# Layer 1's output by rows, and the gates' products back on TensorE, in a four-layer graph network

## The chip, the cores and the metric

The kernel runs on one core of a Trainium2 chip. The metric is the device time of one execution in microseconds, the median of several runs. A core has TensorE (matrix products, PE in the profile), VectorE (DVE), ScalarE (ACT), GpSimd (POOL) and SyncE (SP, which issues transfers). Each engine works through its own instructions in order and waits on semaphores for the others. The on-chip memories are SBUF, for operands, and PSUM, into which TensorE writes its sums.

## The reference

Sixteen graphs (B) with 1024 nodes (N) of 128 features (D), each with a dense 1024 x 1024 adjacency of zeros and ones, go through four layers with residual sums and layer norms between them. Cut to what matters here:

```python
# layer 0: graph attention with one gate
h = x @ W_w.T + W_b
e = (h @ A) @ h.T;  e = e + e.T
att = softmax(where(adj > 0, e, -9e15), axis=1) * adj
hp = relu(att @ h)
coeff = sigmoid(concat([x, hp]) @ gate_w.T + gate_b)      # gate_w: 1 x 256
x1 = layernorm(x + coeff * x + (1 - coeff) * hp)

# layer 1: the adjacency is thinned row by row (dilation), then three steps
for l in 1, 2, 3:
    agg = adj_d @ h / deg
    out = agg @ Wr_l + h @ Wx_l + b_l
    out = out / max(norm(out, axis=-1), 1e-12) * mask
    h = batchnorm(relu(out), g_l, be_l)                   # over all graphs and nodes
x2 = layernorm(x1 + (concat([h1, h2, h3]) @ Wl + bl) * mask)

# layer 2: graph attention with three gates (ig, fg, og: 1 x 256 each, over concat([x, hp]))
# layer 3: two normalised propagations over adj + I, between ELUs
```

A gate's product over `concat([x, hp])` is the sum of a product of `x` with the first 128 weights and one of `hp` with the last 128.

## The kernel before

The program goes stage by stage over all 16 graphs: layer 0; the dilation; the three steps of layer 1; then layers 2 and 3 together. Within a stage the work of neighbouring graphs is interleaved: while graph b is in its attention, graph b+1 is prepared (`before`) and graph b-1 is finished (`after`). The build then orders each engine's instructions. NT is 8, the number of blocks of 128 nodes; H2 is 2, the number of halves of 512. The adjacency as f32 rows comes in 512 KB transfers through two buffers (`an`).

```python
# helpers: a "half" is one PSUM buffer of 128 x 512; "turned" is a transpose by TensorE
def products(psum, *pairs):                 # output by columns: weights stay, x moves
    for p, c, _ in halves(psum):
        for i, (W, x) in enumerate(pairs):
            nc.tensor.matmul(p, W, x[:, c], start=(i == 0), stop=(i == len(pairs) - 1))   # L765
        yield p, c

def gate(out, x, g, tmp):                   # layer 0's gate product with x
    nc.gpsimd.tensor_tensor(tmp, x, g[:, None, :].to_broadcast([P, NT, P]), op=OP.mult)   # L771
    for n in (64, 32):
        nc.gpsimd.tensor_tensor(tmp[:, :, :n], tmp[:, :, :n], tmp[:, :, n:2 * n], op=OP.add)   # L773
    nc.vector.tensor_reduce(out, tmp[:, :, :32], AX.X, OP.add)                            # L774

def normed(small, r):                       # layer norm: VectorE statistics, GpSimd power, ScalarE scale
    ...
    rstd = power_mhalf(small, mv[:, :, 1], add=LN_EPS, name="ln_rstd")                    # L744
    nc.vector.scalar_tensor_tensor(nb, ...)                                               # L790
    for i in range(NT): nc.scalar.activation(r[:, i, :], r[:, i, :], AF.Identity, ...)    # L792
```

Layer 0, where a graph is prepared in eight parts (`it` = 0 to 7), one to each block of adjacency rows. Turns, products and the gate share two PSUM buffers (`ps_h`):

```python
# each part: adjacency rows to bf16 (L904), checked (L907), turned by TensorE (L911), stored as fp8 (L912)
if it == 1:   xT = turned x
elif it == 3: s.hT = W0T, xT products
elif it == 5:
    s.G = ...
    gate(s.gx, s.xn, gxr, work.tile([P, NT, P], F32, name="r"))
elif it == 7: s.hn = turned hT
...
# attention, per block: pmm = hT . G (L723), mask and maximum (L946), exp (L950),
# hs = hn / sum (L954), acc += hs . em (L957)
# after: pz = 8 products of hpT with gw (L966), co = pz + gx, tanh, mix with x, layer norm
```

Layer 1's output, per graph and step:

```python
def out(self, b):
    oT = work.tile([P, N], F32, name="oT")
    for p, c in products(ps_h, (self.Wx, st.hT), (self.Wr, st.ag)):
        nc.scalar.activation(oT[:, c], p, AF.Identity, bias=self.bcol)                    # L1374
    ...
    for p, c, k in turned(*((ps_a, oT, "acc") if self.l == 2 else (ps_h, oT))):           # L758
        nc.scalar.activation(oT[:, c], p, AF.Square)                                      # L1379
        nc.vector.tensor_reduce(ss[:, k], tiles3(oT[:, c]), AX.X, OP.add)                 # L1380
        turns.append((p, k))
    ...
    rn = power_mhalf(small, ss, floor=1e-24, name="rn")
    ...
    for p, k in turns:
        nc.vector.scalar_tensor_tensor(st.n[:, k, :], tiles3(p), 0.0, half_rows(rn[:, k]), ...)   # L1387
# then keep: n turned (L758), evicted (L1396), statistics (L1397), stored; and for steps one and two
# the adjacency product of n in two parts, hi and lo (L1274), scaled into ag (L1406)
```

Layers 2 and 3: the gates' products with x are VectorE's, three gates by eight blocks:

```python
# before: yT, layer norm of xn, then
xT = wide("xT", 2);  turned xn, copied by ScalarE                                         # L1530
for g in range(3):
    for i in range(NT):
        nc.vector.scalar_tensor_tensor(small.tile([P, P], BF16, name="gtmp"), s.xn[:, i, :], 1.0, l2.gxr[g],
                                       op0=OP.mult, op1=OP.mult, accum_out=s.gx[:, g, i:i + 1])   # L1534
s.hT = W2T . xT;  s.G = As2 . hT;  s.hn = turned hT
...
# after: pg = 8 products of hpT with gw (3 columns, L1586); gt = pg + gb (L1588); gt += gx (L1589); tanh (L1590);
# the gated mix, layer norm; U0 product, two ELUs (L1483 to L1485, L1479 to L1481), U1 product (L1494),
# propagation hi and lo (L1508), prop (L1510), ELU, U2 product, propagation, turned back (L758, L1641), layer norm
```

Of the kernel before, what the change touches and what calls it, by code (L numbers as in the profile page):

```python
# [22 lines left out]
P = 128  # L23
# [616 lines left out]
def fast_kernel(ctx: ExitStack, tc: tile.TileContext, t: dict, out: bass.AP, flag: bass.AP):  # L640
# [34 lines left out]
    bad = consts.tile([P, 2, NT, B], BF16, name="bad")  # L675
# [13 lines left out]
    def row_bcast(pool, src, n, name):  # L689

        v = pool.tile([P, n], F32, name=name)
        nc.sync.dma_start(v, bass.AP(tensor=src.tensor, offset=src.offset, ap=[[0, P], [1, n]]))
        return v
# [6 lines left out]
    def matrix(pool, src, name):  # L700
        v = pool.tile([P, P], F32, name=name)
        nc.sync.dma_start(v, src)
        return v
# [63 lines left out]

    def gate(out, x, g, tmp):


        nc.gpsimd.tensor_tensor(tmp, x, g[:, None, :].to_broadcast([P, NT, P]), op=OP.mult)  # L771
        for n in (64, 32):
            nc.gpsimd.tensor_tensor(tmp[:, :, :n], tmp[:, :, :n], tmp[:, :, n:2 * n], op=OP.add)  # L773
        nc.vector.tensor_reduce(out, tmp[:, :, :32], AX.X, OP.add)  # L774
# [100 lines left out]
    with ExitStack() as ph:  # L875
# [11 lines left out]
        gxr = row_bcast(wts, t["L0_gnn_gate_w"][0, :P], P, "l0gxr")  # L887
        gw = column(wts, t["L0_gnn_gate_w"][0, P:], "l0gw")
# [6 lines left out]
        def before(s, b):  # L895
# [3 lines left out]
            for it in range(NT):  # L899
# [13 lines left out]
                if it == 1:  # L913
                    xT = work.tile([P, N], F32, name="xT")
                    for p, c, _ in turned(ps_h, s.xn):
                        nc.scalar.copy(xT[:, c], p)
                elif it == 3:
                    s.hT = work.tile([P, N], F32, name="hT", bufs=2)
                    for p, c in products(ps_h, (W0T, xT)):
                        nc.scalar.activation(s.hT[:, c], p, AF.Identity, bias=b0)  # L920
                elif it == 5:
                    s.G = work.tile([P, N], F32, name="G", bufs=2)
                    for p, c in products(ps_h, (As0, s.hT)):
                        nc.scalar.copy(s.G[:, c], p)
                    s.gx = small.tile([P, NT], F32, name="gx")
                    gate(s.gx, s.xn, gxr, work.tile([P, NT, P], F32, name="r"))
                elif it == 7:
                    s.hn = work.tile([P, N], F32, name="hn")
                    for p, c, _ in turned(ps_h, s.hT):
                        nc.vector.tensor_copy(s.hn[:, c], p)  # L930
# [29 lines left out]
        def after(s, b):  # L960
# [4 lines left out]
            for i in range(NT):  # L965
                nc.tensor.matmul(pz[:, i:i + 1], hpT[:, i * P:(i + 1) * P], gw, start=True, stop=True)  # L966
# [205 lines left out]
    class Layers23:  # L1172
# [8 lines left out]
        def weights(self, ps_h):  # L1181
# [7 lines left out]
            self.gxr = []  # L1189
            self.gw = wts.tile([P, 3], F32, name="l2gw")  # L1190
            self.gb = wts.tile([P, 3], F32, name="l2gb")
            for i, n in enumerate(("ig", "fg", "og")):
                w, src = t[f"L2_gnn_{n}_w"], t[f"L2_gnn_{n}_b"]
                self.gxr.append(row_bcast(wts, w[0, :P], P, f"l2gxr{i}"))
                nc.sync.dma_start(self.gw[:, i:i + 1], bass.AP(tensor=w.tensor, offset=w.offset + P, ap=[[1, P], [1, 1]]))
# [31 lines left out]
    with ExitStack() as ph:  # L1227
# [50 lines left out]
        class Step:  # L1278


            def __init__(self, l, before):
                s = str(l + 1)
                self.l = l
                self.Wr = matrix(wts, t[f"L1_gnn_Wr{s}"], f"Wr{s}")
                self.Wx = matrix(wts, t[f"L1_gnn_Wx{s}"], f"Wx{s}")
                self.bcol = column(wts, t[f"L1_gnn_b{s}"], f"b{s}")
# [8 lines left out]
            def take_norm(self):  # L1295
# [4 lines left out]
                pc = ps_h.tile([P, 1], F32, name="pc", tag="h")  # L1300
                nc.tensor.matmul(pc, ws, ab[:, 1:2], start=True, stop=True)
                nc.vector.tensor_add(self.bcol, self.bcol, pc)
# [66 lines left out]
            def out(self, b):  # L1369

                st = self.batches[b]
                oT = work.tile([P, N], F32, name="oT")
                for p, c in products(ps_h, (self.Wx, st.hT), (self.Wr, st.ag)):
                    nc.scalar.activation(oT[:, c], p, AF.Identity, bias=self.bcol)  # L1374
                yield
                ss = small.tile([P, NT], F32, name="ss")
                turns = []
                for p, c, k in turned(*((ps_a, oT, "acc") if self.l == 2 else (ps_h, oT))):
                    nc.scalar.activation(oT[:, c], p, AF.Square)  # L1379
                    nc.vector.tensor_reduce(ss[:, k], tiles3(oT[:, c]), AX.X, OP.add)  # L1380
                    turns.append((p, k))
# [4 lines left out]
                for p, k in turns:  # L1386
                    nc.vector.scalar_tensor_tensor(st.n[:, k, :], tiles3(p), 0.0, half_rows(rn[:, k]),  # L1387
# [70 lines left out]
    with ExitStack() as ph:  # L1458
# [54 lines left out]
        def before(s, b):  # L1513
# [14 lines left out]
            xT = wide("xT", 2)  # L1528
            for p, c, _ in turned(ps_h, s.xn):
                nc.scalar.copy(xT[:, c], p)  # L1530
            s.gx = small.tile([P, 3, NT], F32, name="gx")
            for g in range(3):
                for i in range(NT):
                    nc.vector.scalar_tensor_tensor(small.tile([P, P], BF16, name="gtmp"), s.xn[:, i, :], 1.0, l2.gxr[g],  # L1534
                                                   op0=OP.mult, op1=OP.mult, accum_out=s.gx[:, g, i:i + 1])
            yield
            s.hT = wide("hT", 2)
            for p, c in products(ps_h, (W2T, xT)):
# [40 lines left out]
        def after(s, b):  # L1579
# [4 lines left out]
            for i in range(NT):  # L1584
                c = slice(i * P, (i + 1) * P)
                nc.tensor.matmul(pg[:, i, :], hpT[:, c], gw, start=True, stop=True)  # L1586
            gt = small.tile([P, NT, 3], F32, name="gt")
            nc.vector.tensor_add(gt, pg, gb[:, None, :].to_broadcast([P, NT, 3]))  # L1588
            nc.vector.tensor_add(gt, gt, s.gx.rearrange("p g t -> p t g"))  # L1589
# [104 lines left out]
```

## Time and profile before

Three runs took 3134.86 us in the median (3132.97 to 3136.49). The profiled execution spans 3134.6 us.

| engine | busy us | share | instructions |
|---|---|---|---|
| TensorE | 2829.4 | 90% | 14162 |
| VectorE | 2348.1 | 75% | 6659 |
| ScalarE | 2077.4 | 66% | 3489 |
| GpSimd | 408.1 | 13% | 340 |

The stages by time: layer 0 until about 777 us, the dilation until about 1195, layer 1's steps until about 1590, 1792 and 1900, layers 2/3 until the end.

How to read it: the shares are averages over stages with different limits, so a stage's own window counts. A line number belongs to the kernel before and may be that of a helper, used in several stages; the tile names tell which. "Idle before" is the time the engine stood still just ahead of that group, with what ended the wait. A mean duration overlaps the next instruction's, so the distance between two starts is the better measure of what one costs in a dense row. An f32 product shows as two records, a turn or a product in a shorter type as one. "Granted clock" is the share of full speed that TensorE was given.

### The profile page before, as it was taken

How to read it: one execution, taken by the hardware profiler on the slowest of the kernel's cores; microseconds unless marked ns; L12 is line 12 of the kernel's file. 1: busy time of each engine (PE TensorE's matmuls, PEld its weight loads, DVE VectorE, ACT ScalarE, POOL GpSimd, SP SyncE). 2: the span in 40 equal slices, each digit the busy share in tenths (PEclk: the TensorE clock that was granted, in tenths of full speed). 3: DMA queues.
4: the chain of work that ended last, by engine and by line, in shares of the span. 5: the costliest groups of instructions: out<-in, count | busy, mean ns of one | idle time of the engine just before them, and what ended most of it. 6: DMA issues, size and time to landing. Idle time of an engine off the chain costs nothing. (4 is left out here: it accounts for less than half of the span.)

```text
span 3134.6 us, 41488 instructions
## 1 busy us (share of the span) xinstructions
PE 2829.4 (90%) x14162; PEld 1715.1 (55%) x14162; DVE 2348.1 (75%) x6659; ACT 2077.4 (66%) x3489; POOL 408.1 (13%) x340
## 2 busy tenths in 40 slices
PE   6998888997899998999999998999999998988995
PEld 3444444443566565777777754555555555555554
DVE  7888888886899994665676666777777777777765
ACT  5777767775678876666666555666666666666653
POOL 1111111113000001111122231000100001100000
PEclk9999999998899999999999998999999999999997
DMA  5344344431000006223366692111111121111000
GB/s 171 131 132 150 118 135 154 134 128 42 1 2 2 2 2 234 81 81 131 125 220 234 227 347 76 34 58 58 67 56 62 62 70 54 54 54 54 21 14 22
DMA packets 123277, 297.94 MB, mean 95 GB/s; under 512 B 12592, under 2 KB 64688, under 8 KB 115888
## 3 DMA queue, kind: packets, MB, share of 16 engines
q1 hardware_dynamic: 102448, 211.20, 20.3%
q0 software_dynamic: 20608, 84.00, 7.5%
q8 instruction: 114, 1.87, 0.2%
q14 instruction: 107, 0.88, 0.1%
HBM read 211.10 MB, written 84.02 MB: 94 GB/s over the span
## 5 line engine op out<-in xcount | busy, mean ns | idle before, releaser
L723 PE MATMUL pmm<-G,hT 128*128 128x512 f32 x1024 | 499.7, 606 | 32.3 <-DVE mx L946 21.6
L792 ACT ACTIVATE xn<-xn,ln_nb,ln_rstd 128x128 f32<-128x128 f32 x512 | 209.1, 481 | 122.7 <-DVE ln_nb L790 122.1
L723 PEld LDWEIGHTS pmm<-G,hT 128*128 128x128 f32 x1024 | 177.2, 191 | 200.7 <-issue 115.3
L1576 PE MATMUL acc<-em,hs 128*128 128x512 f32 x512 | 248.1, 599 | 25.9 <-DVE hs L1573 24.2
L957 PE MATMUL acc<-em,hs 128*128 128x512 f32 x512 | 248.1, 607 | 25.4 <-DVE hs L954 14.1
L744 POOL TENSOR_TENSOR ln_rstd<-ln_rstd,mhalf 128x8 f32<-128x8 f32 x64 | 117.0, 1828 | 1093.1 <-DVE nmx L1564 598.9
L1274 PE MATMUL acc<-a,lo 128*128 128x512 f32 x768 | 238.1, 394 | 2.4 <-DVE lo L1242 2.4
L1274 PE MATMUL acc<-a,hi 128*128 128x512 f32 x768 | 238.1, 395 | 1.7 <-ACT a L1263 1.7
L1134 ACT ACTIVATE q<-s,negc 128x512 f16<-128x512 f32 x256 | 170.3, 693 | 65.8 <-issue 29.3
L1132 PE MATMUL s<-step,carry 128*128 128x512 bf16 (+2 forms) x1088 | 210.3, 306 | 3.5 <-DVE carry L1102 3.2
L907 DVE SCALAR_TENSOR_TENSOR chk<-an 128x1024 fp8e4<-128x1024 f32 x128 | 157.1, 1228 | 60.3 <-DMA an<-in_adj 54.7
L943 ACT ACTIVATE msk<-carry,l0nbig 128x1024 bf16<-128x1024 fp8e4 x128 | 145.1, 1141 | 70.2 <-DVE mx L946 54.9
L1146 ACT ACTIVATE carry<-pc,negone 128x512 fp8e4<-128x512 f32 x256 | 166.4, 693 | 37.8 <-PE pc L1145 26.7
L1557 ACT ACTIVATE msk<-A,nbig 128x1024 bf16<-128x1024 fp8e4 x128 | 145.7, 1140 | 51.0 <-DVE mx L1562 49.9
L904 ACT ACTIVATE ab<-an 128x1024 bf16<-128x1024 f32 x128 | 134.7, 1053 | 61.5 <-PE pt L911 42.3
L946 DVE CUSTOM_DVE_ANT_0 em<-pmm,msk 128x1024 f32<-128x1024 f32 x128 | 155.6, 1216 | 25.6 <-PE acc L957 24.2
L1562 DVE CUSTOM_DVE_ANT_0 em<-pmm,msk 128x1024 f32<-128x1024 f32 x128 | 155.2, 1212 | 20.0 <-PE acc L1576 17.1
L957 PEld LDWEIGHTS acc<-em,hs 128*128 128x128 f32 x512 | 92.2, 192 | 141.5 <-issue 79.1
L1274 PEld LDWEIGHTS acc<-a,lo 128*128 128x128 f32 x768 | 142.9, 188 | 39.9 <-DVE lo L1242 10.1
L950 ACT ACTIVATE em<-em,nmx 128x1024 f32<-128x1024 f32 x128 | 146.0, 1141 | 25.9 <-DVE nmx L948 25.2
L1576 PEld LDWEIGHTS acc<-em,hs 128*128 128x128 f32 x512 | 91.1, 190 | 126.1 <-issue 76.5
L912 DVE TENSOR_SCALAR carry<-pt 128x1024 fp8e4<-128x1024 bf16 x128 | 155.2, 1214 | 4.6 <-PE pt L911 3.9
(281 smaller groups left out, 6459.7 us busy)
## 6 DMA issues: line engine op xcount, KB each, us to landing
an<-in_adj SPq DMA_DIRECT2D x128, 512.0 KB, 3.7
adj_d<-carry POOLq DMA_DIRECT2D x16, 1024.0 KB, 5.0
A<-dil_d SPq DMA_DIRECT2D x16, 1024.0 KB, 6.0
rdeg<-rdeg_d SPq DMA_DIRECT2D x32, 512.0 KB, 4.3
ag_d<-ag POOLq DMA_DIRECT2D x32, 512.0 KB, 5.3
ag<-ag_d SPq DMA_DIRECT2D x32, 512.0 KB, 5.6
A<-adj_d SPq DMA_DIRECT2D x16, 1024.0 KB, 4.8
xn<-in_x SPq DMA_DIRECT2D x16, 512.0 KB, 4.2
```

Of the source, the lines that this page charges most:

```text
L723: nc.tensor.matmul(p[:, h * 512:(h + 1) * 512], lhsT, rhs[:, h * 512:(h + 1) * 512], start=True, stop=True)
L792: nc.scalar.activation(r[:, i, :], r[:, i, :], AF.Identity, scale=rstd[:, i:i + 1], bias=nb[:, i:i + 1])
L907: nc.vector.scalar_tensor_tensor(chk, an, 0.0, an, op0=OP.is_gt, op1=OP.not_equal, accum_out=other[:, c:c + 1], saturate=False)
L912: nc.vector.tensor_scalar(Y[b][:, :, it * P:(it + 1) * P], pt, 0.0, None, op0=OP.is_gt, saturate=False)
L946: nc.vector.tensor_tensor_reduce(em, e, msk, 1.0, -3.0e38, op0=OP.add, op1=OP.max, accum_out=mx)
L957: nc.tensor.matmul(s.acc[:, c], hs, em[:, c], start=(jt == 0), stop=(jt == NT - 1))
L1132: nc.tensor.matmul(s[:, lo or 0:], y, twos if lo is None else step[:, :512 - lo], start=(j == 0), stop=(j == len(terms) - 1))
L1134: nc.scalar.activation(q[:, h * 512:(h + 1) * 512], s, AF.Abs, bias=st.negc[:, i:i + 1])
L1146: nc.scalar.activation(Y[b][:, hb, ks], pc, AF.Relu, bias=negone, saturate=False)
L1274: nc.tensor.matmul(acc, part[:, jt, :], pieces[h * NT // 2 + i][:, j, :], start=(jt == 0 and p == 0), stop=(jt == NT - 1 and p == 1))
L1562: nc.vector.tensor_tensor_reduce(em, e, msk, 1.0, 0.0, op0=OP.add, op1=OP.max, accum_out=mx)
L1576: nc.tensor.matmul(s.acc[:, c], hs, em[:, c], start=(jt == 0), stop=(jt == NT - 1))
```

## The change

Layer 1's output is made by rows at once: each block of 128 nodes of hT and of ag is the operand that stays, and Wx and Wr move, so that the result already has nodes on partitions and needs no turning. The bias then varies along the free axis, so VectorE adds a row of it that is spread over all partitions; the batch norm's shift is folded into that row. Square and sum of squares go through the same PSUM buffer. The gates' products with x, which GpSimd (layer 0) and VectorE (layer 2) made in the kernel before, are TensorE products again, from xT: in layer 0 after the product with W0T, with a copy of 128 x 8 by VectorE; in layer 2 in one sum with the products of hpT, with no addition of gx.

```diff
-    bad = consts.tile([P, 2, NT, B], BF16, name="bad")
+    bad = consts.tile([P, 2, NT, B], F32, name="bad")
...
# layer 0, before
                     for p, c in products(ps_h, (W0T, xT)):
                         nc.scalar.activation(s.hT[:, c], p, AF.Identity, bias=b0)
+                    pz = ps_h.tile([P, NT], F32, name="pz", tag="h")
+                    for i in range(NT):
+                        nc.tensor.matmul(pz[:, i:i + 1], xT[:, i * P:(i + 1) * P], gw[:, 0:1], start=True, stop=True)
+                    s.gx = small.tile([P, NT], F32, name="gx")
+                    nc.vector.tensor_copy(s.gx, pz)
                 elif it == 5:
...
-                    s.gx = small.tile([P, NT], F32, name="gx")
-                    gate(s.gx, s.xn, gxr, work.tile([P, NT, P], F32, name="r"))
...
# layer 1, the batch norm before folded into the bias
-                pc = ps_h.tile([P, 1], F32, name="pc", tag="h")
-                nc.tensor.matmul(pc, ws, ab[:, 1:2], start=True, stop=True)
-                nc.vector.tensor_add(self.bcol, self.bcol, pc)
+                pc = ps_h.tile([P, P], F32, name="pc", tag="h")
+                nc.tensor.matmul(pc, ab[:, 1:2].to_broadcast([P, P]), ws, start=True, stop=True)
+                nc.vector.tensor_add(self.brow, self.brow, pc)
...
# layer 1, out
-                oT = work.tile([P, N], F32, name="oT")
-                for p, c in products(ps_h, (self.Wx, st.hT), (self.Wr, st.ag)):
-                    nc.scalar.activation(oT[:, c], p, AF.Identity, bias=self.bcol)
+                o = work.tile([P, NT, P], F32, name="o", tag="oT")
+                banks = []
+                for p, _, blocks in halves(ps_h):
+                    banks.append(tiles3(p))
+                    for i, j in enumerate(blocks):
+                        for n, (x, W) in enumerate(((st.hT, self.Wx), (st.ag, self.Wr))):
+                            nc.tensor.matmul(p[:, i * P:(i + 1) * P], x[:, j * P:(j + 1) * P], W,
+                                             start=(n == 0), stop=(n == 1))
+                    nc.vector.tensor_add(o[:, blocks[0]:blocks[-1] + 1, :], tiles3(p),
+                                         self.brow[:, None, :].to_broadcast([P, 4, P]))
                 yield
                 ss = small.tile([P, NT], F32, name="ss")
-                turns = []
-                for p, c, k in turned(*((ps_a, oT, "acc") if self.l == 2 else (ps_h, oT))):
-                    nc.scalar.activation(oT[:, c], p, AF.Square)
-                    nc.vector.tensor_reduce(ss[:, k], tiles3(oT[:, c]), AX.X, OP.add)
-                    turns.append((p, k))
+                for h, sq in enumerate(banks):
+                    k = slice(4 * h, 4 * h + 4)
+                    nc.scalar.activation(sq, o[:, k, :], AF.Square)
+                    nc.vector.tensor_reduce(ss[:, k], sq, AX.X, OP.add)
...
-                for p, k in turns:
-                    nc.vector.scalar_tensor_tensor(st.n[:, k, :], tiles3(p), 0.0, half_rows(rn[:, k]),
+                for h in range(H2):
+                    k = slice(4 * h, 4 * h + 4)
+                    nc.vector.scalar_tensor_tensor(st.n[:, k, :], o[:, k, :], 0.0, half_rows(rn[:, k]),
                                                    op0=OP.max, op1=OP.mult)
...
# layer 2, before
-            for g in range(3):
-                for i in range(NT):
-                    nc.vector.scalar_tensor_tensor(small.tile([P, P], BF16, name="gtmp"), s.xn[:, i, :], 1.0, l2.gxr[g],
-                                                   op0=OP.mult, op1=OP.mult, accum_out=s.gx[:, g, i:i + 1])
...
# layer 2, after
-                nc.tensor.matmul(pg[:, i, :], hpT[:, c], gw, start=True, stop=True)
+                nc.tensor.matmul(pg[:, i, :], s.xT[:, c], gw[:, 0, :], start=True, stop=False)
+                nc.tensor.matmul(pg[:, i, :], hpT[:, c], gw[:, 1, :], start=False, stop=True)
...
-            nc.vector.tensor_add(gt, gt, s.gx.rearrange("p g t -> p t g"))
```

Left out of the diff: loading the gates' weights in columns in place of rows spread over partitions, loading the layer 1 bias as such a row, and two buffers for each of layer 1's weights.

## The prediction

> **What bounds the kernel now.** I read the page's busy shares first, then the table of time windows, one window to a stage, then the groups of instructions by line, the chain of waits, and last the timeline of one batch in each stage.
>
> ```profile
> PE 2829.4 (90%) x14162; PEld 1715.1 (55%) x14162; DVE 2348.1 (75%) x6659; ACT 2077.4 (66%) x3489; POOL 408.1 (13%) x340
> ```
>
> TensorE is the busiest engine, but 90% is an average over stages. The windows (start:end, length, busy us and count of each engine, granted clock, DMA share) are, from above: layer 0; layer 1's first, second and third step; layers 2/3.
>
> ```profile
> core 0: us, PE busy (x) PEld busy (x) DVE busy (x) ACT busy (x) POOL busy (x), PEclk, DMA share, GB/s
> 60.00:720.00 660.00, 592.46 (x2515) 299.25 (x2514) 559.57 (x1312) 492.92 (x801) 110.38 (x85) 0.99 0.41 135
> 1215.00:1575.00 360.00, 357.43 (x1637) 254.62 (x1636) 223.31 (x368) 227.12 (x292) 60.75 (x73) 1.00 0.32 111
> 1615.00:1780.00 165.00, 165.00 (x738) 121.24 (x737) 116.91 (x198) 110.34 (x147) 41.15 (x40) 1.00 0.66 228
> 1800.00:1895.00 95.00, 86.82 (x383) 50.99 (x382) 61.32 (x129) 53.82 (x93) 35.25 (x31) 1.00 0.84 306
> 2060.00:2955.00 895.00, 814.23 (x2991) 483.64 (x2990) 656.63 (x2442) 580.79 (x1125) 80.97 (x48) 0.98 0.17 56
> ```
>
> Steps one and two of layer 1 are TensorE and nothing else (357 of 360, 165 of 165): what leaves it there is time saved. Layer 0 (592 of 660) and layers 2/3 (814 of 895) have gaps, so there a chain through other engines sets part of the period. The costs come from these groups (line, engine, count | busy us, mean ns | idle before):
>
> ```profile
> L765 PE MATMUL ph<-hT,Wx 128*128 128x512 f32 x192 | 98.7, 598 | 0.0
> ...
> L1534 DVE SCALAR_TENSOR_TENSOR gtmp<-xn,l2gxr 128x128 bf16<-128x128 f32 x384 | 90.2, 288 | 0.6 <-ACT xn L792 0.6
> ...
> L1494 PE MATMUL ph<-U,ehi 128*128 128x128 f32 x512 | 83.5, 327 | 51.5 <-DVE ehi L1481 48.3 <-DVE ehi L1485 1.9 <-DVE yn L1594 1.3
> ...
> L1586 PE MATMUL pg<-l2gw,hpT 128*128 128x3 f32 x256 | 29.5, 247 | 0.0
> ```
>
> An f32 product is two records here (192 for 48 batches of two halves), a turn is one. In the timeline of layer 1, columns start and length, the products and the turns of oT follow each other without a gap:
>
> ```profile
> 1407.14 1.02 PE L765 MATMUL ph<-ag,Wr 128*128 128x512 f32 x2
> 1408.00 1.91 PE L758 MATMUL ph<-identf,n 128*128 128x128 f32 x16
> 1409.74 1.04 PE L758 MATMUL ph<-identf,oT 128*128 128x128 f32 x8
> ```
>
> Starts are 0.86 apart for two 512-column records: 0.43 each. In layers 2/3 the chain of waits (start, length, what) runs through VectorE's gate products and on into TensorE:
>
> ```profile
> 2455.00 0.84 DVE gtmp L1534 x8
> 2455.85 1.21 DVE zlo L1499 x2
> 2457.05 2.55 DVE gtmp L1534 x24
> ```
>
> [...] L1586 has only 3 moving columns, yet its 16 records take 1.70 us to the next group's start (106 ns each); L1494, with 128, takes 1.78 for 16 (111 ns). [...] 128x512 is 685 to 690 ns from PSUM (L1406, L1510) and 687 from SBUF (L1499). So the last multiply of `out` gains nothing by reading SBUF. [...]
>
> ```profile
> 417.06 2.35 POOL L771 TENSOR_TENSOR r<-xn,l0gxr 128x1024 f32<-128x1024 f32 x1 [15.62 <-issue]
> ```
>
> ```profile
> 418.23 1.27 DVE L954 TENSOR_SCALAR hs<-hn,rs 128x128 f32<-128x128 f32 x1
> ```
>
> hs lasts 1.27 us beside that GpSimd product, 0.28 elsewhere, and TensorE waits 0.41 for it.
>
> **Part 1, layer 1 by rows.** Removed per batch and step: 8 records of 512 columns (8 x 0.43 = 3.44; the chain of waits has 3.44 too) and 8 turns of oT (0.87). Added: 8 blocks x 2 operands x 2 records = 32 of 128 columns at 0.111 = 3.55. Net 3.55 - 4.31 = -0.76 us of TensorE. ScalarE loses the two evictions with bias (687 ns each), VectorE gets the two bias additions from PSUM (about 0.69 each, a pitch of 0.60); Square, sum and last multiply stay. VectorE goes in step one from 62% to about 68%. In step two its 117 of 165 is 8.9 us per 12.5 us batch; with 1.2 to 1.4 more against 11.7 us it is near 87%: still behind TensorE, so I take 0.7 of the 0.76. In step three the period is 5.79 us (start of one batch's products to the next) with a wait of 0.25 for VectorE's n; TensorE would fall to about 4.7, but VectorE rises from 3.7 to about 5.2 and the DMA share is already 0.84, so only about 0.4 comes out. Sum: 16 x 0.76 + 16 x 0.7 + 16 x 0.4 = 30, less about 2 for the step boundaries (the folded bias is now 128x128): **-28 us**.
>
> **Part 2, layers 2/3: 24 gate products per batch leave VectorE.** They start 0.21 apart: 24 x 0.213 = 5.1 us. TensorE gets 8 f32 products with 3 columns: 16 x 0.106 = 1.70. What lies on the path? The chain of waits carries all 5.1 us of them between 2448.05 and 2459.60. But ScalarE runs beside without a gap in that stretch (from 2446.82: normalising, ELU, two exponentials, zhi, xT), so not all comes back. I laid the changed build's order on each engine over the measured durations. The second ELU result is ready at about 2452.1 instead of 2453.0; zhi moves ahead of the second exponential in ScalarE's order; the first propagation starts near 2455.0 instead of 2456.2[...]: -1.9. The new products follow the turns of prop. TensorE is off the path there: the chain goes prop, casts of A, layer norm, ScalarE, gates (2409.9 to 2425.1), and TensorE has waits of 0.50 and 0.57 in it that swallow the added 1.70 nearly whole; about 0.15 is left. Net -1.75 in each of 14 periods (batches 2 to 15 are prepared beside an attention) = -24.5; about -2 in the start-up, where the first two batches' gate products stand alone on VectorE; +2 in the tail, where 1.7 more TensorE stands before the last gates. Sum **-25 us**.
>
> **Part 3, layer 0.** GpSimd loses 4.4 us per batch (2.41 + 2 x 1.02) of no chain; VectorE loses a sum of 0.41 and about 0.5 of blocked hs (mean 340 ns here against 283 in layers 2/3, x 8), and gains a copy of about 0.17. TensorE gains 8 f32 products of one column, 1.7 us, and they take one of two PSUM buffers that the adjacency's turns need. Period: 675 us / 15 = 45.0 us, TensorE busy 40.4 of it. Some of its gaps are waits for VectorE and for adjacency rows from DMA, so part of 1.7 is absorbed: I take +0.9 net, x 16 = **+14 us**. This is my least certain term.
>
> Sum: 3134.9 - 28 - 25 + 14 = **3096 us** (-1.2%).
>
> **Rivals.** (a) Layers 2/3 are really bound by TensorE: then 14 to 16 x 1.70 = +24 to +27 in place of -25, total near 3147. For it: 91% busy and one added engine load; against: the gaps before L1494 (51.5 us in all, nearly all on VectorE's ehi) and the gate products in the chain. (b) VectorE becomes the bound of layer 1's second and third step: part 1 shrinks to about -12, total 3112. For it: the 87% above and in-order waits for GpSimd's power; against: TensorE has no gap there now and loses the wait for oT. (c) Layer 0 absorbs all: [...]0 or less: 3080. (d) All of 5.1 us comes back in layers 2/3: 14 x 3.2 = -45: 3075. For it: the chain as shown; against: ScalarE's gapless stretch.
>
> **Range and chances.** (a) alone would put it at +0.4%, (c) and (d) together near 3060. I give 3062 to 3128. Faster by over 2% needs 3072 or less, that is (c) and (d) nearly whole: 0.20. Slower by over 2% needs more than 62 us lost, which no sum of the parts gives: 0.03.
>
> **What would show it.** Right: TensorE's products in `out` 3.5 us per batch with no turns of oT; periods near 23.6, 11.8 and 5.4 us in layer 1's steps; 72.4 instead of 74.2 in layers 2/3, with the gap before U1's products down from 3.4 to about 2.8 and no wait of propagation for xT; hs at 0.28 everywhere; layer 0's period 45 to 46. Wrong: a 128-column product well over 0.111 us when its weights alternate between hT and ag; TensorE gaps on VectorE's n or o in layer 1; a layers-2/3 period of 75 or more; a layer 0 that grows by the whole 1.7 us or more per batch.

## The result: 0.5% faster, less than half of what was forecast

| | before | after |
|---|---|---|
| median | 3135.68 us (3132.97 to 3137.22) | 3118.57 us (3112.95 to 3124.53) |
| ratio | | 0.9947, 95% interval 0.9926 to 0.9967 |

The whole change was run once more later, on another chip, beside the kernel before (after_again below): 0.9926 (0.9897 to 0.9955). Forecast was 3096, a ratio of 0.988.

**The profile after.** First the groups of instructions that answer to those shown of before (line, engine, operation | busy us, mean ns | idle before and its releasers). The output of layer 1 is now L1373, U1's products are L1496, the gates of layers 2/3 L1583 (x) and L1584 (hpT).

```profile
L1373 PE MATMUL ph<-Wx,hT 128*128 128x128 f32 x768 | 154.1, 283 | 6.5 <-DVE l2WT L709 3.2 <-ACT nT L1398 2.9 <-ACT hT L1354 0.2
L1373 PE MATMUL ph<-Wr,ag 128*128 128x128 f32 x768 | 152.0, 281 | 3.4 <-DVE ag L1361 1.9 <-DMA ag<-ag_d 1.6
...
L1496 PE MATMUL ph<-U,ehi 128*128 128x128 f32 x512 | 73.0, 299 | 42.5 <-DVE ehi L1483 39.5 <-DVE ehi L1487 1.9 <-DVE yn L1591 1.1
...
L1584 PE MATMUL pg<-l2gw,hpT 128*128 128x3 f32 x256 | 48.8, 261 | 0.0
L1583 PE MATMUL pg<-l2gw,xT 128*128 128x3 f32 x256 | 47.0, 254 | 0.0
```

U1's products wait 42.5 us in all instead of 51.5: VectorE has been relieved. The products of `out` wait little themselves (6.5 and 3.4 us in all). The same windows as before (length, busy PE, PEld, DVE, ACT, POOL, granted clock, DMA share, GB/s): layer 0, then step one, two, three of layer 1, then two halves of layers 2/3.

```profile
60.00:720.00 660.00, 628.00 (x2782) 334.08 (x2781) 554.14 (x1321) 496.22 (x806) 52.51 (x44) 0.98 0.39 135
1210.00:1560.00 350.00, 339.06 (x1808) 263.51 (x1807) 232.53 (x383) 201.47 (x253) 56.99 (x72) 1.00 0.30 106
1610.00:1770.00 160.00, 160.00 (x977) 140.71 (x977) 134.46 (x228) 93.37 (x119) 36.73 (x40) 1.00 0.67 234
1800.00:1890.00 90.00, 73.88 (x553) 67.42 (x553) 74.10 (x149) 31.15 (x57) 32.99 (x29) 0.92 0.84 303
2060.00:2500.00 440.00, 410.08 (x1598) 249.81 (x1596) 307.55 (x944) 287.93 (x558) 41.34 (x25) 0.98 0.18 60
2500.00:2950.00 450.00, 419.24 (x1599) 256.37 (x1598) 308.30 (x950) 292.51 (x568) 42.53 (x26) 0.96 0.16 51
```

In layer 0 TensorE is busy 628 of 660 us where it was 592. In step one it has got gaps (339 of 350), and in step three it is busy 74 of 90 us, where it was 87 of 95 before.

**Where the time went.** The stages' lengths, from the starts of the last store of each stage (last x store of layer 0, layer 1's first load of x, last h0T, h1T and h2T, last output). The second pair are profiles from one chip (before_again and after_again):

| stage, us | before | after | before_again | after_again |
|---|---|---|---|---|
| layer 0, from the start | 773.7 | 762.8 | 774.6 | 759.8 |
| dilation | 421.9 | 423.2 | 424.3 | 425.7 |
| layer 1, step one | 393.4 | 401.1 | 395.2 | 400.3 |
| layer 1, step two | 202.7 | 195.0 | 202.7 | 195.0 |
| layer 1, step three | 107.1 | 111.9 | 107.1 | 110.7 |
| layers 2/3, to the last output | 1228.3 | 1215.8 | 1224.9 | 1207.1 |

Layer 1, for which 28 us were forecast, gains nothing in sum; layer 0, for which a loss was forecast, gains; layers 2/3 gain less or more by the run.

**What stalls step one.** The period of a batch is 24.4 us in the first half before and 24.0 after; in the second half it is 24.8 before and 25.6 to 25.7 after. This is TensorE's timeline in a batch of the second half of after (start, length, what, and the wait ahead of it):

```profile
1423.40 0.39 PE L1373 MATMUL ph<-Wr,ag 128*128 128x128 f32 x2
1423.62 1.04 PE L758 MATMUL ph<-identf,n 128*128 128x128 f32 x8
1426.32 1.07 PE L758 MATMUL ph<-identf,n 128*128 128x128 f32 x8 [1.66 <-issue]
```

And VectorE beside it:

```profile
1422.04 0.69 DVE L1375 TENSOR_TENSOR o<-ph,b 128x512 f32<-128x512 f32 x1 [1.96 <-PE ph L1373]
1425.21 0.27 DVE L1345 TENSOR_REDUCE nodeg<-d 8x1 f32<-8x128 f16 x1 [2.48 <-DMA d<-row]
1425.42 0.20 DVE L1347 TENSOR_SCALAR d<-d 8x128 f32<-8x128 f16 x1
1425.55 0.67 DVE L1382 TENSOR_REDUCE ss<-ph 128x4 f32<-128x512 f32 x1
1426.15 0.93 DVE L1348 RECIPROCAL d<-d 8x128 f32<-8x128 f32 x1
1427.01 0.62 DVE L1375 TENSOR_TENSOR o<-ph,b 128x512 f32<-128x512 f32 x1
```

`out`'s first PSUM bank comes free with the sum L1382. That sum stands in VectorE's order behind `nodeg`, which waits 2.48 us for a DMA of 2 KB (the row of degrees). The wait itself is not new. Before, in the same half, VectorE waits for the row even longer:

```profile
1433.95 0.27 DVE L1350 TENSOR_REDUCE nodeg<-d 8x1 f32<-8x128 f16 x1 [4.98 <-DMA d<-row]
```

and TensorE goes on beside it without a gap:

```profile
1431.52 1.02 PE L765 MATMUL ph<-ag,Wr 128*128 128x512 f32 x2
1432.38 1.91 PE L758 MATMUL ph<-identf,n 128*128 128x128 f32 x16
```

There ScalarE's eviction (L1374) frees the products' bank, and it does not stand behind that row. What is new is that a bank hangs on the wait. The row is late in the second half, where a load of 1 MB (A, 1420.15) is issued 1 us ahead of it: the row lands 3.8 to 4.1 us after its issue there and 1.5 us in the first half, where no such load precedes it and L1345 goes without a stall (the first two batches apart).

### The profile page after: what moved, and what is told of

Same layout as the page of the kernel before. It is cut to its first block, busy times and chain, and to the rows that moved or that the text cites. A ratio compares the mean times of both kernels' runs of the same rounds, so it can differ in the third digit from the quotient of the medians.

```text
span 3117.9 us, 43208 instructions
## 1 busy us (share of the span) xinstructions
PE 2857.3 (92%) x15442; PEld 1841.9 (59%) x15442; DVE 2332.4 (75%) x5971; ACT 2016.4 (65%) x3393; POOL 327.2 (10%) x292
## 4 chain that ended last, share of the span: by engine, by line
PE 56%; DVE 21%; issue 5%; ACT 4%; POOL 4%; DMA 3%; SPq 0%; POOLq 0%; DVEq 0%; ACTq 0%
PE acc L1269 9%; PE ph L1510 7%; PE pmm L723 7%; PE acc L1573 5%; PE acc L953 4%; PE ph L765 4%; PE ph L758 4%; PE ph L1373 4%; PE s L1128 3%; POOL ln_rstd L744 3%; DVE ln_st L777 2%; PE ph L1496 2%; DVE mid L1082 2%; PE acc L1246 2%; DVE keep L1132 1%
## 5 line engine op out<-in xcount | busy, mean ns | idle before, releaser
L723 PEld LDWEIGHTS pmm<-G,hT 128*128 128x128 f32 x1024 | 183.7, 195 | 179.8 <-issue 135.7
L1573 PE MATMUL acc<-em,hs 128*128 128x512 f32 x512 | 247.4, 598 | 22.0 <-DVE hs L1570 20.5
L953 PE MATMUL acc<-em,hs 128*128 128x512 f32 x512 | 255.2, 624 | 11.4 <-DVE hs L950 8.7
L1269 PEld LDWEIGHTS acc<-a,hi 128*128 128x128 f32 x768 | 141.6, 188 | 33.8 <-ACT a L1258 1.3
```

The costliest lines, as they stand in the source:

```text
L723: nc.tensor.matmul(p[:, h * 512:(h + 1) * 512], lhsT, rhs[:, h * 512:(h + 1) * 512], start=True, stop=True)
L953: nc.tensor.matmul(s.acc[:, c], hs, em[:, c], start=(jt == 0), stop=(jt == NT - 1))
L1269: nc.tensor.matmul(acc, part[:, jt, :], pieces[h * NT // 2 + i][:, j, :], start=(jt == 0 and p == 0), stop=(jt == NT - 1 and p == 1))
L1573: nc.tensor.matmul(s.acc[:, c], hs, em[:, c], start=(jt == 0), stop=(jt == NT - 1))
```

## The experiments

Ratios are to the kernel before, run beside each kernel on the same chip.

### One part alone

rows_only is the kernel before with the part of the diff on layer 1; the gates stay.

> The kernel before with layer 1's rows alone; the gates stay where they were. Independent parts (my reading of the two traces): step one +7.7 us, step two -7.6, step three +4.7, so about +5 in all: near 3140 us. The prediction on record would give -28: 3107. Rival (the slower step one comes from something the gates changed, such as the placement of tiles in SBUF): -10 to -28. The 512-column products on the adjacency: 0.2335 us apart if the rows cause the longer pitch, 0.2267 as before if they don't.

Measured: 0.9967 (0.9955 to 0.9978), 10 us. Steps 400.5, 196.7 and 108.5 us: layer 1 as expected, the total not. The adjacency products have the longer pitch here too. So the rows cause both, and something outside layer 1 gains.

l0_gate_only is the kernel before with layer 0's gate products on TensorE.

> The kernel before with layer 0's gate products on TensorE alone. By the two traces layer 0 ends 10.9 us earlier: 3125 us, period 44.4, TensorE's waits for mx, carry and hs cut to less than half. The prediction on record: +14, so 3149. Rival (the gain in layer 0 is given back later, at the boundary to the dilation): layer 0 ends 11 us earlier and the total moves by less than 4.

Measured: 0.9961 (0.9944 to 0.9977), that is -12 us, where +14 was forecast. TensorE's idle time in the window of layer 0 (60 to 720) falls from 67 to 37 us.

l23_gates_only is the kernel before with the gates of layers 2/3 on TensorE.

> The kernel before with the gate products of layers 2/3 on TensorE alone. By the two traces -12.5: 3123 us, period near 70.9. The prediction on record: -25, so 3110. Rival (layers 2/3 bound by TensorE there): +24.

Measured: 0.9978 (0.9963 to 0.9994), -7 us: right in sign, a quarter of the size.

### Layer 0: relief against cost

l0_no_x leaves x's share of layer 0's gate out altogether (from l0_gate_only):

```diff
-nc.tensor.matmul(pz[:, i:i + 1], xT[:, i * P:(i + 1) * P], gw[:, 0:1], ...)
-nc.vector.tensor_copy(s.gx, pz)
-nc.vector.tensor_add(co, pz, s.gx)
+nc.vector.tensor_copy(co, pz)
```

> The kernel before with x's share of layer 0's gate left out altogether (neither GpSimd and the sum on VectorE nor TensorE). If TensorE's 1.7 us per batch cost what was predicted, this beats layer 0's gate on TensorE (ratio 0.9961) by some 16 us or more: 0.990. If TensorE takes them in its gaps, it beats it by less than 6: 0.994 to 0.996.

Measured: 0.9913 (0.9895 to 0.9932), -27 us. TensorE's products therefore cost 27 - 12 = 15 us, 0.9 per batch, the term of the prediction (the two intervals leave some 7 to 23; layer 0 takes 768.7 us in the profile of l0_gate_only and 747.7 in this one, 21 apart). What it lacked is the 27 us of relief.

l0_gpsimd_beside is l0_gate_only with GpSimd's three instructions still running, their result unused and VectorE's sum gone:

```diff
+r = work.tile([P, NT, P], F32, name="r")
+nc.gpsimd.tensor_tensor(r, s.xn, gxr[:, None, :].to_broadcast([P, NT, P]), op=OP.mult)
+for n in (64, 32):
+    nc.gpsimd.tensor_tensor(r[:, :, :n], r[:, :, :n], r[:, :, n:2 * n], op=OP.add)
```

> Layer 0's gate on TensorE, with GpSimd's multiply and its two additions left running beside it, their result unused and the sum on VectorE gone. If the gain of layer 0 (12 us) comes from GpSimd no longer standing in VectorE's way, it is lost again here: hs 1.27 us beside the GpSimd product, ratio near 1.000. If it comes from the sum on VectorE and the order of the streams, the gain stays: ratio 0.996.

Measured: 1.0009 (0.9999 to 1.0020). The gain is gone. Groups of hs, first of l0_gate_only:

```profile
L958 DVE TENSOR_SCALAR hs<-hn,rs 128x128 f32<-128x128 f32 x116 | 32.5, 280 | 0.9
```

then of l0_gpsimd_beside:

```profile
L963 DVE TENSOR_SCALAR hs<-hn,rs 128x128 f32<-128x128 f32 x114 | 43.4, 381 | 0.9
```

GpSimd's work of 4.4 us per batch, on no chain itself, costs 15 us (0.9 per batch). VectorE's instructions beside it take longer (hs 381 ns in the mean instead of 280; by what way GpSimd lengthens them, no run shows); that they are what TensorE waits for is read from the trace of before (the 0.41 us for hs), not varied by itself. The other 12 of the 27 us go with the sum on VectorE and the place of the gate in the order of the streams; no run parts these two.

### Layers 2/3: relief against cost

l23_no_x leaves x's share out of the gates of layers 2/3 (from l23_gates_only; the hpT products alone fill pg).

> The kernel before with x's share of the gates of layers 2/3 left out altogether (24 VectorE products per batch gone, no TensorE product added, so the gates get hpT's share alone). It shows what the relief of VectorE is worth by itself. Theory (relief as predicted or more, TensorE's half-speed windows as before): period 71.5 to 72.4 against 74.2, about -28 to -38 us, so a ratio near 0.990, granted clock of layers 2/3 near 0.975. Rival (the relief itself is worth only the 7 us that the gates alone brought): ratio near 0.998.

Measured: 0.9929 (0.9911 to 0.9947), -22 us. l23_both has TensorE's products and VectorE's 24 as well, x counted twice.

> The kernel before with TensorE's x products of the gates of layers 2/3 added while VectorE's 24 stay (x's share is counted twice). It shows what the 1.7 us of TensorE cost by themselves. Theory (TensorE's load brings more windows of half speed): granted clock near 0.955 instead of 0.975 and +15 to +25 us, ratio 1.005 to 1.008. Rival (the added products fit in gaps and the clock does not move): ratio 1.000 to 1.002.

Measured: 1.0124 (1.0101 to 1.0146), +39 us: more than either theory. By the ratios the relief is worth 22 us, near the forecast, and TensorE's products cost 15 beside the relief and 39 without it, where the forecast had 4. The profiles lie closer together. Layers 2/3 take 1201.6 us in l23_no_x, 1228.4 in l23_gates_only (a run 7 us above that kernel's median), 1256.1 in l23_both, and 1225 to 1228 in before: 27 us for the products beside the relief and 28 to 31 without it. Another 11 us of l23_both's profile lie in layer 0 (784.7 against 773.7), where nothing was changed. Why the products cost so much is seen in the starts of the outputs. Those of l23_no_x:

```profile
2131.37 0.94 POOL L1636 DMA_DIRECT2D out<-xn  x1 [3.72 <-ACT xn L792]
2202.86 0.93 POOL L1636 DMA_DIRECT2D out<-xn  x1 [3.72 <-ACT xn L792]
2276.53 0.93 POOL L1636 DMA_DIRECT2D out<-xn  x1 [3.72 <-ACT xn L792]
2349.34 0.93 POOL L1636 DMA_DIRECT2D out<-xn  x1 [3.72 <-ACT xn L792]
```

and those of l23_gates_only:

```profile
2128.54 0.94 POOL L1637 DMA_DIRECT2D out<-xn  x1 [3.72 <-ACT xn L792]
2201.86 0.93 POOL L1637 DMA_DIRECT2D out<-xn  x1 [3.72 <-ACT xn L792]
2276.80 0.93 POOL L1637 DMA_DIRECT2D out<-xn  x1 [3.72 <-ACT xn L792]
2353.93 0.93 POOL L1637 DMA_DIRECT2D out<-xn  x1 [3.72 <-ACT xn L792]
```

Periods of 71.5, 73.7, 72.8 against 73.3, 74.9, 77.1. But the best periods of both kernels are alike, 71.5 and 71.6: then the new products cost nothing, as forecast. The long ones hold pieces at half clock. In this stage the granted clock is 1 or a half, and the pieces at a half are 3.41 or 6.83 us long. This is the piece in the 77.1 us period of l23_gates_only, with the 3.41 us ahead of it (clock is the third figure from the end):

```profile
2266.80:2270.21 3.41, 3.41 (x28) 2.93 (x26) 3.41 (x20) 2.74 (x3) 0.00 (x0) 1.00 0.05 19
2270.21:2277.04 6.83, 6.83 (x21) 4.65 (x21) 1.71 (x7) 4.96 (x11) 1.88 (x2) 0.50 0.42 155
```

and TensorE's timeline there (what is left out are more of the gates' products and a turn):

```profile
2266.96 1.02 PE L723 MATMUL pmm<-G,hT 128*128 128x512 f32 x2
2267.82 0.28 PE L1580 MATMUL pg<-l2gw,xT 128*128 128x3 f32 x2
...
2270.19 0.53 PE L1581 MATMUL pg<-l2gw,hpT 128*128 128x3 f32 x2
...
2273.18 4.68 PE L723 MATMUL pmm<-G,hT 128*128 128x512 f32 x6
```

l23_no_x has half as many gate products in the same place, and full clock after them:

```profile
2267.54 1.84 PE L1580 MATMUL pg<-l2gw,hpT 128*128 128x3 f32 x16
```

```profile
2270.00:2276.00 6.00, 5.60 (x19) 2.65 (x18) 3.96 (x13) 4.20 (x10) 1.64 (x1) 1.00 0.50 176
```

Ahead of the piece the records show TensorE busy throughout, but they have few columns: of those that start in the 3.41 us, 23 have 3, one 128 and two 512, which is 1221 columns. By the distance of 0.226 us between records of 512 columns in the propagation of before (zlo, eight from 2463.98 to 2465.79), 15 of them would start in that time, with 7680 columns (an estimate). Between 2060 and 2960, 10 of the 14 pieces of l23_gates_only and 12 of the 19 of l23_both follow such a stretch, with 19 to 30 records of the gates' products in it. The others, and all pieces of before (11) and l23_no_x (7), follow 3.41 us of which TensorE worked 1.75 us or less: the wait for VectorE ahead of U1's products. So the relief takes pieces of the one kind away, and the products bring pieces of the other.

Over 2060 to 2960 the clock withheld (slices of 6 us, length times what the clock lacks) is 22 us in before (18.8 in before_again), 15 in l23_no_x, 39 in l23_gates_only and 44 in l23_both. It changes from run to run: 23.8 and 15.3 in the two profiles of the whole change, whose layers 2/3 differ by 8.7 us (1215.8 and 1207.1). Over the 22 runs of l23_gates_only the time goes with the mean clock: the quickest, 3122.5 us, has 0.971, the longest, 3156.1 us, 0.961.

### Step one: the row of degrees

A8_after_row ties the next 1 MB load to the row: GpSimd copies 8 numbers of the row into the tile, and the load then overwrites them. The load at its old place is gone, but for the first of them; cut to the lines added:

```diff
 nc.gpsimd.dma_start(d16, row)
+A = wide_pool.tile([P, NT, N], FP8, name="A8", bufs=4)      # of the next batch
+nc.gpsimd.tensor_copy(A.bitcast(F32)[:NT, 0, :1], d16[:, :1])
+nc.sync.dma_start(A.bitcast(F32), dil8_d[b + 1])
```

> The changed kernel, but in step one's second half the 1 MB load of the next adjacency starts only when the row of degrees has landed (a GpSimd copy of 8 numbers from that row into the tile ties them together; the load then overwrites them). If TensorE's 1.6 us wait per batch there comes from VectorE standing in order behind that row while it holds the PSUM banks: the period of the second half falls from 25.7 to about 24.0 and the time by about 8 x 1.6 = 12 us to 3106. Rival (the load disturbs the products themselves, or the second half is slow for another reason): period still above 25, 3116 to 3120.

Measured: 0.9914 (0.9887 to 0.9941). Its six runs go from 3101.5 to 3135.6 us with the mean clock (0.969 to 0.956; 46 us withheld between 2060 and 2960 in the profiled one, the longest), so the ratio says little here. Step one itself is plain: the period is 24.0 us in both halves, up to the twelfth batch. VectorE at the place shown above:

```profile
1420.32 0.27 DVE L1350 TENSOR_REDUCE nodeg<-d 8x1 f32<-8x128 f16 x1 [0.22 <-DMA d<-row]
```

The wait is 0.22 us instead of 2.48. Then come two periods of 27.5 and 29.7. In the first of them step two's own loads of 1 MB begin (L1316), a microsecond ahead of the row:

```profile
1513.51 0.32 SPq L1316 DMA_DIRECT2D A<-dil_d  x1
```

```profile
1514.77 0.51 POOL L1344 DMA_DIRECT2D d<-row  x1 [8.54 <-ACT row L1342]
1520.02 0.17 POOL L1348 CAST A<-d 8x1 f32<-8x1 f16 x1 [4.74 <-issue]
```

The copy waits 4.74 us for the row there, against 1.17 a batch earlier. The cause shows itself twice: take the load away from the row and the stall goes, put one back and it returns. For that reason the tie alone shortens step one by only 2 us (398.9).

### The longer pitch of the adjacency products

The rows don't touch the 512-column products on the adjacency, yet these go 0.2335 us apart after and 0.2267 before. The rows' bias tiles had moved the working tiles: hi and lo, the weights of these products, lie at 384 within 512 bytes after and at 480 before. pad96 moves them back with an unused tile:

```diff
+wts.tile([P, 24], F32, name="pad")
 work = ph.enter_context(tc.tile_pool(name="l1_work", bufs=2))
```

> The changed kernel with an unused tile of 96 bytes ahead of layer 1's working tiles, which puts hi and lo (the weights of the 512-column adjacency products) back at the offset within 512 bytes that they had before (480 instead of 384). If the longer pitch of those products (0.2335 us after, 0.2267 before) comes from where the tiles lie: 0.2267 again, which is 96 records x 16 batches x 0.0068 = 10 us: ratio near 0.991. If it comes from something else in the rows: 0.2335 still, ratio 0.994 to 0.996.

Measured: 0.9945 (0.9931 to 0.9959). The ratio is that of the other theory, but the pitch decides: it is back, the period is 23.64 instead of 24.0 in step one's first half, and step one is six us shorter (394.7). The profiled run had a mean clock of 0.961, and 39 us of clock withheld in layers 2/3. The timeline of pad96 (two records per line):

```profile
1426.85 0.62 PE L1270 MATMUL acc<-a,hi 128*128 128x512 f32 x2
1427.31 0.61 PE L1270 MATMUL acc<-a,lo 128*128 128x512 f32 x2
1427.76 0.62 PE L1270 MATMUL acc<-a,hi 128*128 128x512 f32 x2
1428.21 0.62 PE L1270 MATMUL acc<-a,lo 128*128 128x512 f32 x2
```

Starts are 0.45 to 0.46 apart; in after they are 0.46 to 0.47. In columns_in_step3 the tiles happen to lie at 416, and the pitch (0.229) and the period (23.75) there are in between. The padding moves all working tiles of layer 1; of what these products touch, only hi and lo have moved. Step two gained nothing by the padding (195.6 us), which cast_to_act takes up.

### Step three

squares_in_sbuf writes the squares to the tile that takes n later, so that the bank is free after the bias addition:

```diff
-nc.scalar.activation(sq, o[:, k, :], AF.Square)
-nc.vector.tensor_reduce(ss[:, k], sq, AX.X, OP.add)
+nc.scalar.activation(st.n[:, k, :], o[:, k, :], AF.Square)
+nc.vector.tensor_reduce(ss[:, k], st.n[:, k, :], AX.X, OP.add)
```

> The changed kernel with the squares written to SBUF (the tile that takes n later) instead of back into out's PSUM banks, so that a bank comes free after the bias addition and not only after Square and sum. If the hold through Square and sum is what makes step one's second half wait and step three irregular: second half near 24.0 instead of 25.7 (-12 us) and step three 107 us or less instead of 112. If the wait is for the addition itself, in order behind the row of degrees: second half still near 25, gain under 5 us.

Measured: 0.9944 (0.9927 to 0.9961). Step three 104.1 us, less than in any version; step one's second half still 25.6. So two different causes: in step three the hold of the banks, in step one the place in VectorE's order.

columns_in_step3 keeps the columns of before in step three only.

> The changed kernel with rows in steps one and two and the columns of before in step three. If the loss in step three (107.1 to 111.9 us) comes from the rows there (VectorE gets the bias additions and becomes the bound): step three back to 107, -5 us against the changed kernel, ratio near 0.993. If it comes from something before it (step two's faster end pulls loads together): step three still 110 to 112, ratio 0.9947.

Measured: 0.9908 (0.9895 to 0.9920), step three 107.05 us at 5.8 per batch. The loss was the rows' own. VectorE's largest idle time in the window of step three of after stands here; every other wait of VectorE there is 2.7 us or less:

```profile
L1385 DVE TENSOR_TENSOR rn<-rn,mf 128x8 f32<-128x8 f32 x13 | 2.1, 162 | 10.4 <-POOL rn L744 10.4
```

In those 80 us (1800 to 1880) VectorE works 65.7 and waits 10.4 in order for GpSimd's power, and TensorE stands idle for 10.8. VectorE is not full, though: in squares_in_sbuf, with the same instructions, it works 70.6 of 80 us (1795 to 1875), and a batch takes 5.7 us in the mean instead of 6.2. So its order and the held banks set the pace together. TensorE's clock is 0.94 in those 80 us and 1.00 with the columns; what that costs no run shows.

### Step two, and the cures together

combo joins the ties, the padding and the columns; step two's 1 MB loads are tied by a GpSimd copy from the h tile of the batch before.

> Four things together on the changed kernel: the 1 MB loads of step one start after the row of degrees; step two's loads of the same kind start only when step two is there; the padding (64 bytes here, for the same offset of 480); columns in step three. Step one near 382 to 385 us instead of 401, step three 107: ratio 0.983 to 0.986 if the padding works, 0.986 to 0.989 if it doesn't.

Measured: 0.9926 (0.9913 to 0.9939). Step one 382.9 us, as expected, step three 106.9; but step two 202.8. The tie itself did that, as the chain of waits in it shows:

```profile
1662.27 6.34 DMA hT<-h0T_d
...
1668.73 0.08 POOL A L1340
...
1668.88 1.68 POOL rn L744
...
1670.58 0.18 DVE rn L1425
```

The small copy stands ahead of the power in GpSimd's order and made it wait for a load.

cast_to_act is pad96 with one of VectorE's four casts of the adjacency on ScalarE in step two.

> The kernel with the padding, and in step two one of VectorE's four casts of the adjacency (0.60 us of pitch) moved to ScalarE. If VectorE with its in-order wait for GpSimd's power sets step two at 11.90 us per batch: TensorE sets it now, 11.71, which is 16 x 0.19 = 3 us of step two (195.6 to about 192.5). If something else sets it (loads, GpSimd's own order): 11.90 still.

Measured: 0.9895 (0.9864 to 0.9926). The period of step two's stores falls from 11.90 to 11.83, not to 11.71, and the step takes 195.1 us. VectorE after the edit, in step two:

```profile
1659.13 0.17 DVE L1386 TENSOR_TENSOR rn<-rn,mf 128x8 f32<-128x8 f32 x1 [1.78 <-POOL rn L744]
...
1665.42 0.69 DVE L1383 TENSOR_REDUCE ss<-ph 128x4 f32<-128x512 f32 x1 [0.67 <-ACT ph L1382]
```

Of the 0.60 us taken from VectorE, most came back as a new wait of 0.67 for the Square, which now stands behind a third cast on ScalarE. That fits VectorE and its in-order waits as what holds step two at 11.8 to 11.9, but TensorE shows no gap in either kernel (busy 119.7 of 120 us in pad96, from 1640 to 1760, and 120.0 here), so it is not shown, and how low step two could go stays open. The better ratio than pad96's isn't owed to step two; the step lengths of the two don't differ by it.

best has the ties (step two's first four loads tied by ScalarE), the padding, the cast, and squares in SBUF in step three.

> All four cures on the changed kernel: step one's 1 MB loads after the row of degrees, and the first four of step two's kept out of step one; the padding; one cast less on VectorE in step two; squares in SBUF in step three. By the single runs: step one 383 us (401 after), step two 192 (195), step three 104 (112), so some 29 us less than the changed kernel: ratio 0.985 to 0.987. Rival (the granted clock of layers 2/3 gives part back, as it seems to in the kernels above): 0.988 to 0.992.

Measured: 3097.85 us, ratio 0.9882 (0.9850 to 0.9914). Step one 383.6, step two 197.2, step three 105.0: 685.8 us for layer 1, where it is 706.1 to 708.0 in the whole change's two profiles and 703.2 to 705.1 in before. Step two is 2 us longer than in after; step two's loads now fall in it. The ratio lies in the range of the rival, and the runs bear it out: three took 3086 to 3087 us at a mean clock of 0.969 to 0.971, three 3109 to 3115 at 0.960 to 0.962. It is faster than before; that it is faster than the changed kernel too is likely from the step lengths, but the two were not run on one chip (0.9926 to 0.9947 there).

### The sum of the parts

before_again is the kernel before, rows_again is rows_only and after_again the whole change, on one chip.

> The kernel before once more, to have its stages on the same chip as the next two. Layer 1's steps 393 to 395, 202.7 and 107.1 us, as in all kernels with columns; ratio 1.000. If layer 0 varies from run to run in the same code: its end anywhere from 770 to 785 us.

Measured: 1.0008 (0.9997 to 1.0020), the steps of layer 1 as expected, layer 0 774.6 us.

> Layer 1's rows alone once more. Layer 1: step one 400 us, step two 196, step three 108 to 109, so 2 to 5 us more than before_again in all. If the ratio of 0.9967 stands (0.995 to 0.998), the gain must be seen in layer 0 or layers 2/3, which have the same instructions in the same order; if it was chance, the ratio is 1.000 to 1.002.

Measured: 0.9972 (0.9962 to 0.9981), 9 us. Layer 1: 395.2 + 202.7 + 107.1 = 705.1 us before, 401.8 + 195.0 + 109.1 = 705.9 with rows: nothing. The gain is layer 0's, 774.6 to 765.4 us, in which the two programs have the same instructions in the same order with the same waits. A single profile doesn't give its size: in the first pair layer 0 went from 773.7 to 770.1, and the five profiles of kernels with the same layer 0 and no rows have 773.7 to 784.7. But the two with rows lie below all of them. What differs is told under the last heading.

> The whole change once more: ratio 0.993 to 0.997; layer 0 ends 10 to 15 us earlier than in before_again, step one +7 us, step two -7.5, step three +4, layers 2/3 -5 to -20 with the granted clock of that run.

Measured: 0.9926 (0.9897 to 0.9955), by stages in the table above. Alone, the parts give -9 to -10 (rows), -12 (layer 0's gate) and -7 (gates of layers 2/3), -28 to -29 in all; the whole change gave -17 in the first measurement and -23 here by the ratio. The f32 `bad` of the diff is in none of the three; the dilation, where it could tell, has 423.2 and 425.7 us with it, and 421 to 426 without.

## Why the prediction was wrong, step by step

**Part 1, layer 1 (-28): wrong, and the largest miss.** The arithmetic of TensorE held: L1373 starts 0.223 apart per pair, 3.57 us per batch against 3.55 forecast, and the turns are gone. Of the signs of being wrong, TensorE's gaps in layer 1 came true. The step that failed is "Steps one and two of layer 1 are TensorE and nothing else: what leaves it there is time saved". Three things took it back. (a) Step one, forecast -12, measured +5 to +8: with the addition the release of the bank moved from ScalarE to VectorE, behind a wait for a small DMA; 1.6 to 1.7 us in each batch of the second half (A8_after_row). (b) Steps one and two: 0.0068 us more on each adjacency product, 64 records per batch in step one, 0.44 us of the 0.76 (pad96). (c) Step three, forecast -6, measured +4 to +5 (and +1 to +2 in the two kernels with rows alone): rival (b) in kind, VectorE's in-order waits with banks held through Square and sum (columns_in_step3, squares_in_sbuf). Step two, forecast -11, gave -7.7; why it stays at 11.90 us and not the 11.8 forecast is open, for the shorter pitch alone did not change it (pad96). VectorE at "62% to about 68%" said nothing of when it would be asked.

**Part 2, layers 2/3 (-25): sign right, size 7.** The relief was sized well, 22 us (l23_no_x), and undisturbed periods are 71.6, better than the forecast 72.4. The mis-sized term is TensorE's 1.70 us, "swallowed nearly whole; about 0.15 is left" plus 2 in the tail, some 4 us: it measured 15. Rival (a) was not right as put, since undisturbed periods show no cost; what costs is the granted clock (39 us withheld in l23_gates_only, 15 in l23_no_x). TensorE's gaps do take in the 1.70 us, but the 32 records of 3 columns in a row are followed by half clock (10 of 14 pieces in l23_gates_only), which the 16 of before were not. Rival (d) is not borne out. Of the -1.9 forecast ahead of the propagation, 1.2 is its earlier start; the other 0.7 was my estimate and isn't shown.

**Part 3, layer 0 (+14): wrong sign.** TensorE's cost, +0.9 per batch, fits (15 us, with a wide interval). The failed term is the other side: I left 0.9 us per batch of VectorE's work (the sum, and hs at 340 ns against 283) in the text and not in the sum. With the sum on VectorE gone, the relief is 27 us. So (c) was right for the gate, -12.

Outside every term: the kernels with rows alone are some 9 us shorter, and their profiles show it in layer 0. That is about half of what the first measurement gave for the whole change.

## What to carry to other kernels

When work moves from one engine to another, ask not only what it costs there but what now stands ahead of it in that engine's order, and which buffers it frees: in step one here a bank that VectorE frees came free only after VectorE's wait of 2.48 us for a DMA of 2 KB. An engine "on no chain" can still cost time: GpSimd's 4.4 us per batch in layer 0 cost 0.9 per batch, 15 us in all. So measure its removal by itself, and count relief and cost as two terms. Look at what a run of small products does to the granted clock behind it, and take the gain in such a stage from several profiles: between 15 and 46 us of clock were withheld in layers 2/3 here, in the same kernel from 15 to 24.

## What the runs showed of the hardware

- The pitch of the 512-column products on the adjacency went with the place of their weights in SBUF: 0.2267 us with hi and lo at 480 within 512 bytes (before, pad96), 0.229 at 416 (columns_in_step3), 0.2335 at 384 (after). Why is open; the moving tile lay at 480 in all.
- In layers 2/3 the granted clock was 1 or 0.5, and the pieces at 0.5 were 3.41 us long or twice that. They came after TensorE's waits and also after stretches of busy records: in all 19 profiles, between 2060 and 2960, each piece follows 3.41 us in which TensorE worked 1.75 us or less, or in which its records are busy throughout with 19 to 30 records of 3 columns among them and no more than 1593 columns in all. The second kind occurs in all eleven profiles of kernels with x's products on TensorE in layers 2/3 and in none of the other eight. What it is in such a stretch that half clock follows is not shown; no run varied the columns alone.
- Layer 0's loads of adjacency land sooner in all kernels with rows in the three steps, in the median 3.3 to 3.4 us after issue, than in all kernels without (3.7 to 3.8); the two with columns in step three lie between (3.6). The part of the program that loads them is the same in all. Of before_again and rows_again (VectorE's group that waits for them in layer 0):

```profile
L907 DVE SCALAR_TENSOR_TENSOR chk<-an 128x1024 fp8e4<-128x1024 f32 x114 | 139.1, 1221 | 52.8 <-DMA an<-in_adj 52.5
```

```profile
L907 DVE SCALAR_TENSOR_TENSOR chk<-an 128x1024 fp8e4<-128x1024 f32 x114 | 139.1, 1220 | 40.2 <-DMA an<-in_adj 39.6
```

The wait for the load is 13 us shorter, which would be enough for the 9 us. What in the program makes the loads quicker wasn't tried.
